# Degrees from the ends of runs instead of 64 counting passes, edge words on GpSimd, two sets of rank words

## The chip, the cores and the metric

The kernel runs on one core of one Trainium2 chip. A core has a matmul engine (TensorE, PE in the profile, with its weight load PEld), a vector engine (VectorE, DVE), a scalar engine (ScalarE, ACT), GpSimd (POOL) and a queue engine (SyncE, SP); 16 DMA engines move data between its on-chip memory and HBM. The metric is the device time of one execution in microseconds.

## The reference

A graph network of two layers runs over 6250 nodes with 128 features and 100,000 edges. Each edge has a source, a destination and one of 32 edge types, each node one of 16 node types. The edges come sorted by destination. `h` starts as `x`; each of the two layers computes

```python
k = typed_linear(h, ntype, Wk).reshape(n, H, HS)     # 16 weight sets, by node type
q = typed_linear(h, ntype, Wq).reshape(n, H, HS)
v = typed_linear(h, ntype, Wv).reshape(n, H, HS)
kT = jnp.einsum('nhd,htdo->nhto', k, Watt)           # 32 edge types
vT = jnp.einsum('nhd,htdo->nhto', v, Wmsg)
a = jnp.einsum('ehd,ehd->eh', kT[src, :, etype], q[dst]) * pri[:, etype].T / SQRT_D
att = edge_softmax(a, dst, n)                        # softmax over the edges of one destination
hag = segment_sum(vT[src, :, etype] * att, dst)
h = layernorm(gated(silu(typed_linear(hag, ntype, Wa)), h))
```

and the output is `layernorm(x + h @ ff_w + ff_b)`. There are 8 heads of 16 features.

## The kernel before

The kernel makes, for each layer, a table in HBM with one row of 256 floats (K and V) for every pair of node and edge type. Then it treats nodes in blocks of 128 with similar degrees: GpSimd gathers, edge slot by edge slot, one table row for each of the 128 nodes (L1310), and VectorE does the softmax and the sums. So three stages follow each other: layer 0's table; layer 0's edges with layer 1's table beside them; layer 1's edges. The change touches the first stage alone.

**Start (L316 to L468).** The edges lie in on-chip tiles of 128 partitions by 782 columns (`dsti`, `srci`, `eti`), partition by partition in their sorted order. The nodes are sorted by type with one-hot words and matmuls (L372 to L431), which gives `inv`, the list by which x is fetched. Beside that, VectorE makes the edge words `kvi = src * 32 + etype` (L448), the word by which a table row is named later, and checks that destinations do not fall along the edges (`falls`, L451 to L455) and that no partition spans 64 or more destinations (L457 to L460). A branch (L575) takes another path for unsorted edges; it isn't taken here. Its condition is read by every engine.

**Layer 0's table.** For each node type in turn (`linears0`, L952) GpSimd fetches blocks of x (L947), TensorE transposes them, ScalarE copies the result, TensorE multiplies by this type's Wk and Wv, and ScalarE and VectorE copy K and V (L991, L989); VectorE also copies what two types share (L971). Then for each block of 128 nodes and each half of the 32 edge types `table_block` (L287) issues eight matmuls of 512 columns, copies each result into a tile `st` (L306 on ScalarE; a quarter on VectorE, L304, in the stages "gathers" and "done"), and GpSimd scatters the tile to the table (L1002): 128 rows of 4096 floats. There are 49 blocks and 98 scatters, and four `st` tiles.

**Ranking, beside the table.** A Python generator, `rank_order` (L644), is advanced between the half-blocks of the table (L1014 to L1030): one step at each half in most stages, three steps in two halves while it yields nothing, and one step in two halves in the stage "gathers". It has these parts:

- `degrees` (L513). Column by column of 64, VectorE compares all 782 destinations less the partition's lowest with a constant and sums the hits (L537, an instruction with an accumulator that is read by a second one). After each four columns the counts are split into two small parts (L543 to L546), and one-hot words are built: `ol` for the node's place in its block (L548), `oh` for its block, times the count parts (L551, L555). Four matmuls a group (L531) sum them over the partitions.
- a histogram of degrees and a serial chain of small steps between VectorE and TensorE (L672 to L766),
- ranks of all nodes, by one-hot words of 128 columns for each block (L781 to L797),
- rank words (L813 to L838): for each group of up to four blocks VectorE builds `ol` (L825), `oh` (L829) and `ov` (L833), and matmuls L837 sum them to what each rank holds. Each of these three tiles exists once.
- the stage "gathers": GpSimd fetches the edge words of each block (L869) and its rows of x (L881), and stores the rows in rank order (L878, L887).

**Order of the work.** GpSimd's instructions run as the program states them. For the other engines a planner orders the instructions by its own estimates, so an instruction of VectorE can stand far ahead of its place in the program; each engine then works strictly in that order and waits at its head.

## Time and profile before

| what | us |
|---|---|
| median of three runs | 3341.53 (3329.39 to 3342.41) |
| the profiled execution | 3345.07 |
| its span, from the first to the last instruction | 3343.3 |
| start to the branch | 0 to 44 |
| layer 0's table, first to last scatter | 60.7 to 637.9 |
| first gather of layer 0's edges | 656.4 |

| from 44 to 656 us | PE | DVE | ACT | POOL |
|---|---|---|---|---|
| busy us | 521.4 | 288.9 | 362.2 | 266.3 |

A row of the timeline has the start and the duration in us, the engine, the line, the operation, the tile written and those read, their shapes, the count, and in brackets how long the engine was idle before it and what ended that wait. A row of a group of instructions has line, engine, operation, tiles, shape and count, then the busy time in us, the mean of one in ns, and the idle time ahead of them. A row of the busy table by stage has the stretch and its length, then for each engine the busy time and the number of instructions, the mean granted clock of TensorE as a share, the mean share of the DMA engines in use, and GB/s moved. "PE busy" counts pipelined matmuls with modelled ends, so a TensorE that is always busy need not be at its peak.

### The profile page before, as it was taken

The page shows a single profiled execution, that of the slowest core. Times are in us where ns is not written, and L with a number is a line of the kernel's source. Part 1 is how long each engine was busy: PE and PEld are TensorE (multiplying, and loading weights), DVE is VectorE, ACT ScalarE, POOL GpSimd, SP SyncE. Part 2 cuts the span into 40 slices and gives each one's busy share as a digit, 9 for nine tenths or more (in the row PEclk, how much of TensorE's full clock was granted, in tenths as well). Part 3 has the DMA queues.
Part 4 walks back from the last instruction along what each step waited for, and adds up shares of the span by engine and source line. Part 5 has one row for each costly group of instructions (what it writes and reads, how often), then busy time and mean ns, then how long its engine had stood idle before and what let it go on. Part 6 is the DMA issues. An engine that isn't in the chain of part 4 may idle for free. (4 is left out here: it accounts for less than half of the span.)

```text
span 3343.3 us, 22057 instructions
## 1 busy us (share of the span) xinstructions
PE 1738.2 (52%) x5612; PEld 808.2 (24%) x5612; DVE 1938.7 (58%) x4025; ACT 1014.6 (30%) x1677; POOL 2159.0 (65%) x2213
## 2 busy tenths in 40 slices
PE   3798998611874678766777677301212122122213
PEld 1344444400332323332332223101101111011111
DVE  8756332146646776666656653246556666666765
ACT  2575655400432235424342355101111121011111
POOL 2233665377577776777677563477767777777773
PEclk9679777555775777777777777655555555555655
DMA  7697999953675667757786588833333333333331
GB/s 200 255 391 304 401 399 406 382 111 101 214 244 196 217 231 285 253 192 248 266 290 217 170 299 341 296 108 104 101 93 103 101 101 101 101 103 99 100 101 44
DMA packets 194482, 691.09 MB, mean 207 GB/s; under 512 B 55469, under 2 KB 106032, under 8 KB 169298
## 3 DMA queue, kind: packets, MB, share of 16 engines
q0 software_dynamic: 119120, 651.15, 55.3%
q1 hardware_dynamic: 58838, 31.29, 3.5%
q10 hardware_dynamic: 16384, 7.11, 1.0%
q8 instruction: 48, 0.79, 0.1%
q14 instruction: 92, 0.75, 0.1%
HBM read 264.91 MB, written 429.48 MB: 208 GB/s over the span
## 5 line engine op out<-in xcount | busy, mean ns | idle before, releaser
L1310 POOL DMA_INDIRECT kv<-tab,ell x1734 | 1734.4, 1000 | 578.6 <-issue 451.5
L306 ACT COPY st<-tb 128x512 f32<-128x512 f32 (+1 forms) x1064 | 722.1, 758 | 396.8 <-PE tb L299 252.2
L284 PE MATMUL nb<-ident,hag 128*128 128x128 f32 x100 | 24.5, 379 | 750.5 <-DVE hag L1358 750.5
L1322 DVE TENSOR_TENSOR kv<-kv,q 128x896 f32<-128x896 f32 (+4 forms) x135 | 136.7, 1014 | 434.8 <-DMA kv<-tab,ell 410.9
L1322 DVE TENSOR_TENSOR kv<-kv,tb 128x768 f32<-128x768 f32 (+4 forms) x134 | 135.9, 1014 | 409.5 <-DMA kv<-tab,ell 356.2
L299 PE MATMUL tb<-bdv,vT 32*128 32x512 f32 x784 | 291.4, 862 | 32.9 <-ACT st L306 23.1
L299 PE MATMUL tb<-bdv,kvT 32*128 32x512 f32 x800 | 268.4, 823 | 53.6 <-ACT st L306 53.1
L299 PE MATMUL tb<-bdk,kvT 32*128 32x512 f32 x800 | 260.6, 818 | 56.1 <-ACT st L306 55.8
L1326 DVE TENSOR_REDUCE a<-kv 128x48 f32<-128x768 f32 (+4 forms) x269 | 269.7, 1003 | 1.5
L1002 POOL DMA_INDIRECT tab<-st,rows x98 | 103.5, 1056 | 240.5 <-ACT st L306 195.6
L278 PE MATMUL nb<-xm,wa 128*128 128x384 f32 (+1 forms) x384 | 201.9, 689 | 103.6 <-DVE xm L269 103.6
L299 PE MATMUL tb<-bdk,kT 32*128 32x512 f32 x784 | 250.9, 850 | 0.0
L1521 POOL DMA_INDIRECT tab<-st,row x100 | 104.2, 1042 | 177.1 <-ACT st L306 121.4
L304 DVE COPY st<-tb 128x512 f32<-128x512 f32 (+1 forms) x120 | 89.0, 744 | 205.3 <-PE tb L299 131.9
L284 PEld LDWEIGHTS nb<-ident,hag 128*128 128x128 f32 x100 | 14.8, 188 | 767.2 <-issue 552.5
L278 PE MATMUL nb<-xm,wq 128*128 128x384 f32 (+1 forms) x192 | 104.4, 705 | 136.0 <-DVE xm L269 136.0
L269 DVE SCALAR_TENSOR_TENSOR xm<-ntb,nb 128x384 f32<-128x384 bf16 (+1 forms) x240 | 132.1, 592 | 40.9 <-PE nb L284 28.0
L1206 ACT ACTIVATE tb<-a 128x128 f32<-128x128 f32 (+15 forms) x50 | 14.5, 289 | 435.8 <-DVE a L1203 435.8
L1454 PE MATMUL nb<-xm,wkqv 128*128 128x384 f32 (+1 forms) x288 | 125.5, 592 | 40.8 <-DVE xm L269 35.4
L278 PEld LDWEIGHTS nb<-xm,wa 128*128 128x128 f32 x384 | 94.0, 255 | 206.5 <-DVE xm L269 123.9
L1473 PE MATMUL nb<-xm,wkqv 128*128 128x384 f32 (+1 forms) x288 | 134.1, 626 | 14.0 <-DVE xm L269 14.0
L299 PEld LDWEIGHTS tb<-bdv,vT 32*128 32x128 f32 x784 | 108.8, 239 | 120.8 <-ACT st L306 92.3
(331 smaller groups left out, 2813.7 us busy)
## 6 DMA issues: line engine op xcount, KB each, us to landing
kv<-tab,ell POOLq DMA_INDIRECT x1734
hr<-xrd SPq DMA_DIRECT2D x21, 192.0 KB, 4.2
xrd<-xr POOLq DMA_DIRECT2D x11, 256.0 KB
hr<-xrd SPq DMA_DIRECT2D x10, 256.0 KB, 5.7
hrd<-hs SPq DMA_DIRECT2D x10, 192.0 KB, 2.2
qrd<-q SPq DMA_DIRECT2D x10, 192.0 KB, 6.8
tab<-st,row POOLq DMA_INDIRECT x100
tab<-st,rows POOLq DMA_INDIRECT x98
```

The source lines that it names most:

```text
L269: nc.vector.scalar_tensor_tensor(xm[:, :n], ntb[:, :n], float(t), hT[:, :n], op0=ALU.is_equal, op1=ALU.mult)
L278: nc.tensor.matmul(ps[:, :n], w[:, t, :], xm[:, :n], start=(t == types[0]), stop=(t == types[-1]))
L299: nc.tensor.matmul(pt[:, b], yT[s, i * P:(i + 1) * P], bd[s, tt, :], start=True, stop=True)
L304: nc.vector.tensor_copy(to, pt)
L306: nc.scalar.copy(to, pt)
L1002: put = nc.gpsimd.indirect_dma_start(out=tabs[0].rearrange("(n t) c -> n (t c)", t=16), out_offset=bass.IndirectOffsetOnAxis(ap=rows1[:, t ...
L1310: get = nc.gpsimd.indirect_dma_start(out=kv[:, j - j0, :], out_offset=None, in_=tabs[l][:], in_offset=bass.IndirectOffsetOnAxis(ap=ell[:, ...
L1322: nc.vector.tensor_tensor(kk, kk, q.unsqueeze(1).to_broadcast([P, c, D]), op=ALU.mult)
L1326: nc.vector.tensor_reduce(a[:, j0:j1, :], kk.rearrange("p k (h d) -> p k h d", h=H), axis=AX.X, op=ALU.add)
L1454: nc.tensor.matmul(outs[j][:, :n], wkqv[:, j, t, :], xm[:, :n], start=(t == types[0]), stop=(t == types[-1]))
L1473: nc.tensor.matmul(ps[:, :n], wkqv[:, j, t, :], xm[:, :n], start=(t == types[0]), stop=(t == types[-1]))
L1521: put = nc.gpsimd.indirect_dma_start(out=tabs[1].rearrange("(n t) c -> n (t c)", t=16), out_offset=bass.IndirectOffsetOnAxis(ap=row2[:, tg ...
```

## The change

It has three parts, all in the first stage.

1. `degrees` looks for the ends of runs. Each edge gets a key, `dst * 1024 + column + 1`; keys of edges whose successor has the same destination become 0. Eight times VectorE takes the eight largest keys of a partition and, but for the last time, replaces them by 0. Of the 64 keys found, the high bits are the nodes, and the differences of the low bits of neighbours are the degrees. They are split once for all, and one-hot words are built from bf16 operands as before, in 16 groups. The generator yields 44 times in this part instead of 35.
2. The edge words and the differences of neighbouring destinations are made on GpSimd in four instructions; VectorE takes the minimum of the differences. Behind the branch GpSimd makes the differences once more (the other path changes `dsti`) and numbers the columns.
3. Rank words have two sets of tiles, taken in turn, and the matmuls of a group are issued after the words of the next.

```diff
-    nc.vector.scalar_tensor_tensor(kvi, srci, float(RT), eti, op0=ALU.mult, op1=ALU.add)
-    falls = pp.tile([P, EC], F32, name="falls", tag="lo")
-    nc.vector.tensor_tensor(falls[:, :EC - 1], dsti[:, :EC - 1], dsti[:, 1:], op=ALU.is_gt)
-    nc.vector.tensor_tensor(falls[:, EC - 1:], dsti[:, EC - 1:], nxt, op=ALU.is_gt)
+    nc.gpsimd.tensor_scalar(kvi, srci, float(RT), None, op0=ALU.mult)
+    nc.gpsimd.tensor_tensor(kvi, kvi, eti, op=ALU.add)
+    rise = pp.tile([P, EC], I32, name="rise", tag="lo")
+    nc.gpsimd.tensor_tensor(rise[:, :EC - 1], dsti[:, 1:], dsti[:, :EC - 1], op=ALU.subtract)
+    nc.gpsimd.tensor_tensor(rise[:, EC - 1:], nxt, dsti[:, EC - 1:], op=ALU.subtract)
     nfalls = pp.tile([P, 2], F32, name="nfalls")
-    nc.vector.tensor_reduce(nfalls[:, 0:1], falls, axis=AX.X, op=ALU.add)
+    nc.vector.tensor_reduce(nfalls[:, 0:1], rise, axis=AX.X, op=ALU.min)
+    nc.vector.tensor_scalar(nfalls[:, 0:1], nfalls[:, 0:1], 0.0, None, op0=ALU.is_lt)
...
     def degrees(got):
-        rel = pp.tile([P, EC], F32, name="rel", tag="lo")
-        nc.vector.tensor_scalar(rel, dsti, lowest, None, op0=ALU.subtract)
...
+        last = pp.tile([P, EC], F32, name="last_at", tag="lo")
+        nc.vector.scalar_tensor_tensor(last, dsti, float(ROOM), nth, op0=ALU.mult, op1=ALU.add)
+        nc.vector.scalar_tensor_tensor(last[:, :EC - 1], rises[:, :EC - 1], 1.0, last[:, :EC - 1],
+                                       op0=ALU.min, op1=ALU.mult)
         yield
+        found = pp.tile([P, NEAR], F32, name="ends")
+        for r in range(0, NEAR, 8):
+            nc.vector.max(out=found[:, r:r + 8], in_=last)
+            if r + 8 < NEAR:
+                nc.vector.match_replace(out=last, in_to_replace=found[:, r:r + 8],
+                                        in_values=last, imm_value=0.0)
+            yield "degrees"
...
-        for c0 in range(0, NEAR, SB):
-            for c in range(c0, c0 + SB):
-                nc.vector.tensor_scalar(same, rel, float(c), None, op0=ALU.is_equal, op1=ALU.add,
-                                        accum_out=near[:, c:c + 1])
-                if c % 2:
-                    yield "degrees"
-            sl = slice(c0, c0 + SB)
-            neari = pp2.tile([P, SB], I32, name="neari")
-            nc.vector.tensor_copy(neari, near[:, sl])
...
+        for c0 in range(0, NEAR, G):
+            sl = slice(c0, c0 + G)
+            ol = pp2.tile([P, G, P], BF16, name="oc")
+            nc.vector.tensor_tensor(ol, at[:, 0, sl].unsqueeze(2).to_broadcast([P, G, P]),
+                                    colb.unsqueeze(1).to_broadcast([P, G, P]), op=ALU.is_equal)
+            yield "degrees"
...
+    rises = pp.tile([P, EC], I32, name="rises", tag="srci")
+    nc.gpsimd.tensor_tensor(rises[:, :EC - 1], dsti[:, 1:], dsti[:, :EC - 1], op=ALU.subtract)
+    nth = pp.tile([P, EC], F32, name="nth", tag="eti")
+    nc.gpsimd.iota(nth, pattern=[[1, EC]], base=1, channel_multiplier=0,
+                   allow_small_or_imprecise_dtypes=True)
...
-            for i0, k in superblocks(NT):
+            def said(i0, k, ol, ov):
+                for i in range(k):
+                    nc.tensor.matmul(say_ps, ol[:, i, :], ov[:, i], start=(i0 + i == 0),
+                                     stop=(i0 + i == NT - 1))
+            ready = None
+            for n, (i0, k) in enumerate(superblocks(NT)):
                 sl = slice(i0, i0 + k)
-                ol = pp2.tile([P, SB, P], F32, name="rl", bufs=1)
+                ol, oh, ov = (
+                    pool.tile([P, SB, *w], F32, name=f"say_{tag}", tag=tag, bufs=1)
+                    for (pool, tag), w in zip(
+                        ((pp, "srci"), (pp, "eti"), (pp, "lo")) if n % 2 else
+                        ((pp2, "rl"), (pp2, "rh"), (pp2, "rv")), ((P,), (NB,), (4, NB))))
...
-                for i in range(k):
-                    nc.tensor.matmul(say_ps, ol[:, i, :], ov[:, i], start=(i0 + i == 0),
-                                     stop=(i0 + i == NT - 1))
+                if ready:
+                    said(*ready)
+                ready = i0, k, ol, ov
                 yield
+            said(*ready)
```

More of the change, by code (lines that the diff above doesn't have):

```diff
@@ L527, in degrees @@
+        nc.vector.tensor_copy(nearb, nears)
+        yield "degrees"
         deg_ps = pps.tile([P, 2, NT], F32, name="ps")
+        G = SB
         def products(c0, ol, oh):
-            for c in range(c0, c0 + SB):
+            for c in range(c0, c0 + G):
                 nc.tensor.matmul(deg_ps, ol[:, c - c0, :], oh[:, c - c0],
@@ L560, in degrees @@
             ready = c0, ol, oh
-        yield "degrees"
+            yield "degrees"
         products(*ready)
```

50 lines of the change are left out of this document (27 added, 23 removed).

## The prediction

> **What bounds the kernel now.** I read the page first, then the busy table by stage, then the scatter issues in the timeline, then the groups of instructions. The page's span, shares and transfer rates:
>
> ```profile
> span 3343.3 us, 22057 instructions
> PE 1738.2 (52%) x5612; PEld 808.2 (24%) x5612; DVE 1938.7 (58%) x4025; ACT 1014.6 (30%) x1677; POOL 2159.0 (65%) x2213
> GB/s 200 255 391 304 401 399 406 382 111 101 214 244 196 217 231 285 253 192 248 266 290 217 170 299 341 296 108 104 101 93 103 101 101 101 101 103 99 100 101 44
> ```
>
> No engine is full over the span, so only the stage that is changed counts: the first eight slices of 83.6 us, where 98 scatters write layer 0's table. Its end is fixed by the last scatter and its landing (L1002), because layer 0's first gather (L1310) waits for it:
>
> ```profile
> L1002 POOL DMA_INDIRECT tab<-st,rows x98: 974/1017/2214, 60.7 to 637.9; - x98
> ...
> 656.38 1.01 POOL L1310 DMA_INDIRECT kv<-tab,ell  x1 [17.55 <-DMA tab<-st,rows]
> ```
>
> From there on the instruction order of the changed program is that of the old one on every engine. So what the stage wins or loses up to 656 us is carried one to one to the end of the span. The stage in four stretches (columns: busy time and count for PE, PEld, DVE, ACT, POOL; then granted clock, DMA share, GB/s):
>
> ```profile
> 61.00:178.00 117.00, 90.66 (x369) 41.08 (x368) 85.05 (x274) 72.30 (x144) 32.64 (x38) 0.71 0.72 295
> 178.00:277.00 99.00, 94.30 (x519) 47.43 (x518) 67.88 (x143) 71.83 (x142) 29.18 (x32) 0.83 0.94 388
> 277.00:318.00 41.00, 35.23 (x167) 19.96 (x165) 27.70 (x92) 22.59 (x44) 11.55 (x11) 1.00 0.62 253
> 318.00:656.00 338.00, 290.33 (x971) 148.29 (x971) 93.55 (x156) 189.69 (x371) 185.62 (x200) 0.67 0.98 396
> ```
>
> The last stretch is bound by the transfers: 396 GB/s at a share of 0.98 makes 404 GB/s when full, and one scatter (128 rows of 4096 floats, 2.10 MB) takes 5.2 us. The transfers stood idle for 0.28 x 117 = 32.8, 0.06 x 99 = 5.9, 0.38 x 41 = 15.6 and 0.02 x 338 = 6.8 us, 61 us in all. That is the most that any work on the stage after the first scatter can win. The first stretch is the counting of degrees, the third the rank words.
>
> In the first stretch four scatters leave between 60.7 and 74.43, 4.6 us apart; then comes a hole, and the DVE row shows why: the copy of the second node type's V (L989), which the next table block needs, stood in the queue behind counting passes.
>
> ```profile
> 55.38 0.69 DVE L989 COPY vT<-l 128x512 f32<-128x512 f32 x1 [0.54 <-PE l L986]
> 74.43 1.01 POOL L1002 DMA_INDIRECT tab<-st,rows  x1 [2.59 <-DVE same_dst L537]
> 88.46 0.69 DVE L989 COPY vT<-l 128x512 f32 x1
> 93.71 1.02 POOL L1002 DMA_INDIRECT tab<-st,rows  x1 [16.51 <-ACT st L306]
> 177.64 0.99 POOL L1002 DMA_INDIRECT tab<-st,rows  x1 [2.17 <-ACT st L306]
> ```
>
> **The change, part by part.** Degrees, removed and added, from the groups of the stage (busy, mean ns, idle before):
>
> ```profile
> L537 DVE TENSOR_SCALAR_CACHE_REDUCE same_dst<-rel 128x782 bf16<-128x782 f32 x64 | 61.6, 963 | 0.7
> L555 DVE TENSOR_TENSOR rhb<-rhb,nears 128x196 bf16<-128x196 bf16 x32 | 11.5, 360 | 0.7
> L548 DVE TENSOR_TENSOR oc<-nidat,colf 128x512 bf16<-128x512 f32 x16 | 11.0, 688 | 15.7 <-PE ps L531 15.6
> L531 PE MATMUL ps<-rhb,oc 128*128 128x98 bf16 x64 | 6.8, 243 | 22.2 <-DVE rhb L555 22.2
> L551 DVE TENSOR_TENSOR rhb<-nidat,colf 128x196 bf16<-128x196 f32 x16 | 5.7, 354 | 0.0
> L537 DVE DVE_READ_ACCUMULATOR same_dst<-rel 128x1 f32 x64 | 5.2, 82 | 0.0
> L543 DVE CAST neari<-near 128x4 int32<-128x4 f32 x16 | 2.9, 182 | 0.3
> ```
>
> Before, VectorE did 61.6 + 5.2 of counting, 11.5 + 11.0 + 5.7 of one-hot words and three small conversions in each of 16 blocks (about 8.5): 103 us. After, it forms the keys in two passes (1.9), makes 8 maxima searches and 7 replacements over the same 782 columns, some 12 small splits (2.0) and the same 16 blocks of words (28.2). Neither search form is in this trace. From below, a pass over 782 columns costs 0.96 (L537); from above, a pass that carries a value from element to element costs 1.78:
>
> ```profile
> 16.02 1.78 DVE L390 TENSOR_TENSOR_SCAN sums_t<-ones,sums_t 128x784 f32<-128x784 f32 x1
> ```
>
> I take 1.0, nearer the counting pass, which also streams all columns and keeps a little: 15 us, 47 in all, 56 us of VectorE work less. Of that only what holds the scatters counts. In the changed order the second type's V copy stands behind all eight searches, the splits and two blocks of words. VectorE gets past the first type's V (the copy at 55.38) at about 57 us, as before; then about 10 us of searches, 2 of splits and 5 of words with copies and dependencies between them (about 2) put that copy at 76 instead of 88.46. The scatter follows 5 us later, at 81 instead of 93.71: **13 us won**. From there to the scatter at 177.64 there were 13 intervals in 83.9 us; without counting they take 13 x 5.2 = 68, or 75 if a half-clocked TensorE shows now and then (below). I take 71: **another 13 won**. The sum of 26 leaves 7 of the 32.8 us of idle transfers, for type changes and the first scatters.
>
> **Rank words.** Before, one block was a closed loop (L825, L833, then the matmuls L837, then L825 again):
>
> ```profile
> 287.18 1.62 PE L837 MATMUL ps<-rv,rl 128*128 128x200 f32 x8 [0.63 <-DVE rv L833]
> 288.73 1.13 PE L299 MATMUL tb<-bdk,kT 32*128 32x512 f32 x4
> 288.84 0.69 DVE L825 TENSOR_TENSOR rl<-partf,colf 128x512 f32<-128x512 f32 x1 [1.31 <-PE ps L837]
> 289.45 0.98 DVE L833 TENSOR_TENSOR rv<-rh,say 128x800 f32<-128x800 f32 x1
> 290.46 0.32 DVE L829 TENSOR_TENSOR rh<-partf,colf 128x150 f32<-128x150 f32 x1
> ...
> 292.03 1.14 PE L299 MATMUL tb<-bdv,vT 32*128 32x512 f32 x8
> ```
>
> With two sets of words and the products one block late, TensorE no longer waits 0.63 in each of 13 blocks: 8.2 us. The table's matmuls are no longer cut into halves there: 13 pieces become 9, and a half costs as much as a whole (1.13 against 1.14): 4.5 us. VectorE's own 0.69 + 0.32 + 0.98 = 2.0 a block, 26 in all, fits below what is left of the 41 us, but shares its queue with type copies. I take **10 us won** of 12.7; ends 4 (only the pieces joined) and 13.
>
> **Edge words and checks on GpSimd.** VectorE loses the passes L448 and L452 at the start, and no longer waits there for the edge types:
>
> ```profile
> 4.63 0.97 DVE L452 TENSOR_TENSOR falls<-dsti 128x781 f32<-128x781 int32 x1 [0.79 <-DMA dsti<-in_dst_dram]
> 11.28 0.97 DVE L448 SCALAR_TENSOR_TENSOR kvi<-srci,eti 128x782 int32<-128x782 int32 x1 [2.02 <-DMA eti<-in_edge_type_dram]
> 14.93 1.03 DVE L389 COPY sums_t<-tb 128x392 f32<-128x392 f32 x2
> 199.13 0.46 POOL L966 MEMSET kT<- 128x382 f32 x1
> ```
>
> But the minimum of the rises waits for GpSimd's last piece, and stands ahead of L389 and of everything that leads to the first fetch of x. GpSimd's price for 782 columns: one stream as the memset has it gives 0.94; two inputs and an output as three such streams give 2.8. I take two streams, 1.9. The Trainium skill (GPSIMD Engine Reference, section 4.1 Engine selection) speaks against this part: elementwise work belongs on VectorE, GpSimd being about twice as slow with two inputs. By its figures (section 3.1) an estimate is 1.7 us a pass, and the sum would not move by 0.5 us; no row here shows such a pass. The edge types land at 11.28, the addition ends at 13.2, the minimum at 14.4: L389 starts 0.5 sooner than now. Behind it VectorE has two blocks of degree words and some splits less, about 1.5 us. After the branch, the rises are made again and columns numbered on GpSimd, ahead of the second fetch of x in its queue: 1.9 + 0.9 = 2.8 later. I count nothing in sum; with the ends 0.94 and 2.8 it is 3 won to 4 lost.
>
> **Moved work at no cost.** The degree part has nine steps more, so ranking ends nine half-blocks later: gathers of edge words and x rows (L869, L881) begin five scatters later and end three scatters before the last, not seven. Their cover is the full transfer queue of the last stretch. If it goes, the wait of the last row store is exposed:
>
> ```profile
> 612.77 0.80 POOL L887 DMA_DIRECT2D xrd<-xr  x1 [8.60 <-DMA xr<-in_x_dram,some]
> ```
>
> Three scatters stand behind it then; the queue held 17.55 us of work after the last scatter, so 8.6 stays covered. SP's and ACT's queues keep their order but for copies.
>
> **Sum.** 13 + 13 + 10 = 36, less 1 for what a fuller transfer queue can no longer take in: 35 us. The profiled execution took 3345.07 and becomes 3310; it lies 3.5 us above the median of the runs shown, so the median becomes 3341.5 - 35 = 3307.
>
> **Rivals.** (a) TensorE's clock falls while it waits for transfers, and the degree stage runs at the half-clock pace:
>
> ```profile
> 132.00:140.00 8.00, 8.00 (x32) 3.71 (x32) 3.02 (x10) 5.67 (x11) 3.52 (x4) 0.50 0.77 312
> 160.00:178.00 18.00, 18.00 (x94) 8.79 (x91) 7.09 (x26) 17.55 (x37) 6.87 (x9) 1.00 1.01 418
> ...
> 131.66 1.01 POOL L1002 DMA_INDIRECT tab<-st,rows  x1 [3.87 <-ACT st L306]
> 137.82 1.01 POOL L1002 DMA_INDIRECT tab<-st,rows  x1 [3.87 <-ACT st L306]
> ```
>
> At clock 0.50 scatters are 6.16 us apart with these degree matmuls between. Thirteen such intervals are 80, not 71: 3316. Against it: a TensorE without a pause got 1.00 again by 160. [...] (b) Transfers never idle behind the first scatter: 58 won, 3283; against it, type changes and the serial steps between ranks stay. (c) Slower: the searches cost more than a pass. Each us on the price delays the second V copy by 15 us. At 1.78 the time is 3319; the gain is gone at 3.3 us a search; at 4.5 the kernel is slower by 0.5%; at 6, 3382. For it: no row prices these forms; against it: every other pass of this width costs 1.8 or less. (d) GpSimd's passes are far slower: above 2.8 us, each us more delays minimum and fetches by about 4.5; at 8 us, 27 are lost and the time is 3334, no measurable change. (e) The change gives nothing because transfers fill the time anyway, 3341: the 0.98 speaks for it, the 0.72 and 0.62 against.
>
> **How the numbers follow.** A run of this kernel can be told from no change beyond about 0.5%, 17 us. Chances: forecast 0.58, (a) 0.16, (b) 0.07, (c) beyond 2 us 0.09, (d) 0.05, (e) 0.05. Faster: the first three and little more, 0.80; the same: (d), (e) and a fringe of (c), 0.11; slower: the rest of (c), 0.09. The range takes (a), (b), and (d) up to no gain: 3283 to 3335; the forecast's own is 3295 to 3320.
>
> **What would show it.** The scatter now at 93.71 at about 81; that at 177.64 near 150; DMA share from 61 to 150 above 0.9; blocks of rank words 2.5 us apart, not 3.3; searches of about 1 us; the first gather of layer 0 at about 621. Wrong: searches over 3 us, a late minimum ahead of the type counting, or a granted clock of 0.5 in the degree stage.

## The result and the profile after

The changed kernel takes 3311.61 us (median of 8 runs, 3301.43 to 3320.38), the kernel before, run beside it, 3340.44 (8 runs, 3329.39 to 3348.8): a ratio of 0.9918, 95% interval 0.9895 to 0.994. That is 28.8 us less by the medians. The profiled execution of the changed kernel took 3308.28, its span fell by 36.8 us. The page of the changed kernel, as for the kernel before:

```profile
span 3306.5 us, 21912 instructions
PE 1715.2 (52%) x5612; PEld 795.9 (24%) x5612; DVE 1890.3 (57%) x3877; ACT 1013.5 (31%) x1677; POOL 2165.7 (65%) x2219
GB/s 172 403 412 340 400 406 411 279 94 103 278 221 194 181 248 285 253 200 258 270 292 177 217 305 312 290 108 104 102 92 103 101 102 101 102 102 99 99 101 44
```

VectorE lost 48.4 us of busy time and TensorE 23.0, and the second slice went from 255 to 403 GB/s. The busy table of the changed kernel over the same four stretches:

```profile
61.00:178.00 117.00, 113.76 (x466) 53.56 (x458) 48.93 (x127) 95.47 (x190) 40.69 (x46) 0.83 0.93 383
178.00:277.00 99.00, 95.23 (x543) 49.49 (x542) 69.84 (x146) 73.92 (x148) 30.60 (x33) 0.88 0.96 397
277.00:318.00 41.00, 35.94 (x174) 22.10 (x174) 31.11 (x103) 23.86 (x48) 15.64 (x16) 0.83 0.74 299
318.00:656.00 338.00, 267.12 (x896) 132.49 (x891) 96.36 (x152) 169.83 (x334) 200.26 (x213) 0.68 0.99 379
```

The DMA share of the first stretch rose from 0.72 to 0.93, of the third from 0.62 to 0.74 only. In bytes, by two rows of the same view for before and then two for the changed kernel:

```profile
61.00:277.00 216.00, 184.96 (x887) 88.50 (x886) 152.93 (x416) 144.13 (x285) 61.82 (x69) 0.76 0.82 338
277.00:350.00 73.00, 61.81 (x271) 32.61 (x271) 43.05 (x121) 41.32 (x81) 30.05 (x30) 0.91 0.73 294
```

```profile
61.00:277.00 216.00, 208.98 (x1008) 103.05 (x1000) 118.78 (x273) 169.39 (x337) 71.28 (x79) 0.85 0.94 390
277.00:350.00 73.00, 64.65 (x296) 36.93 (x296) 42.44 (x121) 46.69 (x92) 37.02 (x40) 0.85 0.86 348
```

By 350 us the kernel before had moved 216 x 0.338 + 73 x 0.294 = 94.5 MB, the changed kernel 84.2 + 25.4 = 109.6 MB. The 15.1 MB between them are 37 us at the 404 GB/s of a full queue: the gain of this pair of profiles (36.8 us of span) is transfers that no longer wait.

Scatters and the first gather in the timeline of the changed kernel (scatters are counted from 0; those that the prediction calls by 93.71 and 177.64 are scatter 4 and scatter 17):

```profile
66.30 1.03 POOL L1036 DMA_INDIRECT tab<-st,rows  x1 [7.35 <-ACT st L308]
...
84.22 1.02 POOL L1036 DMA_INDIRECT tab<-st,rows  x1 [1.44 <-ACT st L308]
...
151.42 1.50 POOL L1036 DMA_INDIRECT tab<-st,rows  x1 [4.27 <-ACT st L308]
...
594.12 0.80 POOL L921 DMA_DIRECT2D xrd<-xr  x1 [8.18 <-DMA xr<-in_x_dram,some]
...
597.85 0.97 POOL L1036 DMA_INDIRECT tab<-st,rows  x1 [0.30 <-issue]
617.90 1.01 POOL L1344 DMA_INDIRECT kv<-tab,ell  x1 [19.08 <-DMA tab<-st,rows]
```

The wait of 16.51 us ahead of scatter 4 is gone (1.44). But scatter 0 starts at 66.30 instead of 60.72. The stage, split at scatters (us, both columns read from the timelines):

| from | to | before | after | won |
|---|---|---|---|---|
| start | scatter 0 | 60.72 | 66.30 | -5.6 |
| scatter 0 | scatter 4 | 32.99 | 17.92 | 15.1 |
| scatter 4 | scatter 17 | 83.93 | 67.20 | 16.7 |
| scatter 17 | scatter 22 | 26.23 | 27.99 | -1.8 |
| scatter 22 | scatter 44 (rank words) | 143.50 | 131.71 | 11.8 |
| scatter 44 | first gather | 309.01 | 306.78 | 2.2 |
| first gather | end of the span | 2686.9 | 2688.6 | -1.7 |

So there are two gains, in the degrees and in the rank words, and one loss that the prediction had put at nothing: the start.

### The profile page after: what moved, and what is told of

Its sections match the earlier page's. It is cut to its first block, busy times and chain, and to the rows that moved or that the text cites. A ratio compares the mean times of both kernels' runs of the same rounds, so it can differ in the third digit from the quotient of the medians.

```text
span 3306.5 us, 21912 instructions
## 1 busy us (share of the span) xinstructions
PE 1715.2 (52%) x5612; PEld 795.9 (24%) x5612; DVE 1890.3 (57%) x3877; ACT 1013.5 (31%) x1677; POOL 2165.7 (65%) x2219
## 5 line engine op out<-in xcount | busy, mean ns | idle before, releaser
L301 PE MATMUL tb<-bdk,kT 32*128 32x512 f32 x784 | 221.3, 836 | 1.6 <-DVE st L306 1.6
L286 PEld LDWEIGHTS nb<-ident,hag 128*128 128x128 f32 x100 | 15.1, 191 | 766.3 <-issue 550.4
L301 PEld LDWEIGHTS tb<-bdv,vT 32*128 32x128 f32 x784 | 116.1, 229 | 127.7 <-ACT st L308 100.0
```

The source lines that it names most:

```text
L301: nc.tensor.matmul(pt[:, b], yT[s, i * P:(i + 1) * P], bd[s, tt, :], start=True, stop=True)
```

## The experiments

All ratios are to the kernel before, run beside the others on the same chip; its median there was 3343.66 us for degrees_only to words_on_vector, 3340.14 for after_again to spread_words and 3348.95 for the last four, so medians of different groups are not compared directly. The stage's times of every profile in one place (us; "rest" is span less first gather; the last columns are the median of all runs of that kernel and its ratio). The names are explained one by one below; after_again is the changed kernel without an edit.

| kernel | scatter 0 | 4 | 22 | 44 | first gather | rest | median | ratio, 95% |
|---|---|---|---|---|---|---|---|---|
| before | 60.72 | 93.71 | 203.87 | 347.37 | 656.38 | 2686.9 | 3340.44 | 1 |
| changed | 66.30 | 84.22 | 179.41 | 311.12 | 617.90 | 2688.6 | 3311.61 | 0.9918 (0.9895 to 0.994) |
| degrees_only | 61.91 | 81.44 | 173.01 | 318.06 | 624.87 | 2691.1 | 3320.55 | 0.9949 (0.9929 to 0.9969) |
| words_only | 60.80 | 93.81 | 204.00 | 334.68 | 643.47 | 2683.1 | 3328.45 | 0.9964 (0.995 to 0.9977) |
| gpsimd_only | 62.33 | 94.52 | 201.13 | 336.71 | 647.85 | 2684.6 | 3338.42 | 0.9997 (0.9983 to 1.0012) |
| words_on_vector | 61.48 | 81.00 | 172.53 | 305.67 | 612.88 | 2690.9 | 3311.49 | 0.9924 (0.9902 to 0.9946) |
| after_again | 66.00 | 83.62 | 181.93 | 320.92 | 628.23 | 2689.0 | 3316.48 | 0.9925 (0.9905 to 0.9945) |
| twice_max | 66.55 | 88.24 | 185.01 | 314.90 | 621.82 | 2684.3 | 3308.90 | 0.9908 (0.9893 to 0.9924) |
| rises_on_vector | 64.38 | 82.01 | 175.60 | 308.68 | 615.32 | 2690.6 | 3308.18 | 0.9914 (0.9889 to 0.994) |
| spread_words | 64.89 | 82.51 | 182.10 | 307.31 | 616.72 | 2683.0 | 3301.52 | 0.9888 (0.987 to 0.9906) |
| rise_only_gpsimd | 64.08 | 81.70 | 179.76 | 318.71 | 625.46 | 2694.1 | 3321.39 | 0.992 (0.99 to 0.9941) |
| edge_words_only_gpsimd | 61.91 | 79.54 | 184.73 | 316.42 | 623.55 | 2687.6 | 3308.26 | 0.9881 (0.9858 to 0.9904) |
| spread_on_vector | 63.14 | 82.52 | 186.50 | 310.41 | 620.38 | 2688.3 | 3305.46 | 0.9867 (0.9844 to 0.9889) |
| spread_all_on_vector | 60.94 | 80.46 | 178.43 | 301.79 | 611.48 | 2688.7 | 3301.99 | 0.9876 (0.9852 to 0.99) |

The rest after the first gather stays within 2683 to 2694 whatever is done to the stage, and follows no edit. Two profiles of one and the same kernel, changed and after_again, differ by 0.3 us at scatter 0 and by 10.3 at the first gather. So a difference of a few us between two single profiles says something at scatter 0, and little at the first gather.

### The three parts one at a time

The kernel before with the degree part alone (rises and column numbers behind the branch included):

```diff
 # the changed kernel, with edge words, the order test and rank words of before
-    nc.gpsimd.tensor_scalar(kvi, srci, float(RT), None, op0=ALU.mult)
-    nc.gpsimd.tensor_tensor(kvi, kvi, eti, op=ALU.add)
+    nc.vector.scalar_tensor_tensor(kvi, srci, float(RT), eti, op0=ALU.mult, op1=ALU.add)
...
-                if ready:
-                    said(*ready)
-                ready = i0, k, ol, ov
+                for i in range(k):
+                    nc.tensor.matmul(say_ps, ol[:, i, :], ov[:, i], start=(i0 + i == 0),
+                                     stop=(i0 + i == NT - 1))
```

> The kernel before with the degree part alone (keys, maxima searches, words from bf16; the two helper instructions behind the branch on GpSimd come with it); edge words stay on VectorE, rank words are single. My theory: the counting passes held the second node type's V copy and starved TensorE, so this part alone brings 24 to 28 us less 3 for the helpers ahead of the fetches: 21 to 25 us faster than before; the scatter number 17 (from 0) near 150 us, but blocks of rank words still 3.3 us apart. Rival, the transfers fill the time anyway: less than 6 us faster. Rival, the parts only win together because transfers then catch up at the rank words: 10 to 15 us.

Measured: 0.9949, 17 us of 3343.66 by the ratio and 23 by the medians, so its theory (21 to 25) and its last rival (10 to 15) can't be told apart by the time; the first rival is out. From scatter 0 to 22 it takes 111.1 us instead of 143.15, 32 less, nearly as the changed kernel (113.1). Scatter 17 leaves at 145.22, sooner than the 150 expected.

The kernel before with the new rank words alone:

```diff
-                ol = pp2.tile([P, SB, P], F32, name="rl", bufs=1)
+                ol, oh, ov = (
+                    pool.tile([P, SB, *w], F32, name=f"say_{tag}", tag=tag, bufs=1)
...
+                if ready:
+                    said(*ready)
+                ready = i0, k, ol, ov
```

> The kernel before with two sets of rank words alone. My theory: TensorE's wait of 0.63 us in each of 13 blocks goes and the table's matmuls are no longer cut: blocks 2.5 us apart instead of 3.3, 8 to 12 us faster than before. Rival, transfers lag there anyway and take the gain back later: 0 to 3 us. Start and degree stage as before.

Measured: 0.9964, 12 us by the ratio, 15 by the medians. All scatters up to the 28th stay where they were; scatter 44 comes 12.7 us sooner, the first gather 12.9.

The kernel before with the four GpSimd instructions at the start alone:

```diff
-    nc.vector.scalar_tensor_tensor(kvi, srci, float(RT), eti, op0=ALU.mult, op1=ALU.add)
+    nc.gpsimd.tensor_scalar(kvi, srci, float(RT), None, op0=ALU.mult)
+    nc.gpsimd.tensor_tensor(kvi, kvi, eti, op=ALU.add)
...
-    nc.vector.tensor_reduce(nfalls[:, 0:1], falls, axis=AX.X, op=ALU.add)
+    nc.vector.tensor_reduce(nfalls[:, 0:1], rise, axis=AX.X, op=ALU.min)
```

> The kernel before with the edge words and the check of order on GpSimd alone. My prediction counted this part at nothing, 3 us won to 4 lost. By the changed kernel's trace the type counting starts at 15.80 instead of 14.93 us behind the minimum, so 1 us slower is what the start alone gives; if the 2.9 us longer branch of the changed kernel (from the condition to the next instruction 4.6 instead of 1.5 us) belongs to this part, 4 us slower. Rival, GpSimd's words free VectorE at the start: 1 to 2 us faster. The degree stage keeps its hole before scatter 4.

Measured: 0.9997, nothing that can be told from no change, with scatter 0 at 62.33 instead of 60.72. By the ratios (1 less ratio, times the kernel before) the parts are 17 + 12 + 1 = 30 us and the whole is 27. By the medians they are 23 + 15 + 5 = 43 against 29, and at the first gather of the profiles 31.5 + 12.9 + 8.5 = 53 against 38.5. So each of the first two parts wins by itself; whether the parts add up isn't shown.

### What the GpSimd part costs at the start

The changed kernel with edge words and order test back on VectorE:

```diff
-    nc.gpsimd.tensor_scalar(kvi, srci, float(RT), None, op0=ALU.mult)
-    nc.gpsimd.tensor_tensor(kvi, kvi, eti, op=ALU.add)
+    nc.vector.scalar_tensor_tensor(kvi, srci, float(RT), eti, op0=ALU.mult, op1=ALU.add)
...
-    nc.gpsimd.tensor_tensor(rise[:, :EC - 1], dsti[:, 1:], dsti[:, :EC - 1], op=ALU.subtract)
...
+    nc.vector.tensor_tensor(falls[:, :EC - 1], dsti[:, :EC - 1], dsti[:, 1:], op=ALU.is_gt)
...
```

> The changed kernel with one part undone: edge words and the check of order back on VectorE. If GpSimd's words cost the start about 1 us and nothing else, it is 0 to 2 us faster than the changed kernel (31 us faster than before); if the longer branch belongs to GpSimd's words, 4 us faster than the changed kernel. Rival, they win what they take off VectorE: 1 to 2 us slower than the changed kernel. Either way the degree and word parts alone keep nearly the whole gain.

Measured: scatter 0 at 61.48, 4.8 us sooner, and the first gather 5.0 sooner, but a median of 3311.49 (0.9924): within the spread of runs this is the changed kernel's own time. 5 us are 0.15%, less than these medians tell apart. Type counting starts at 14.45 (15.80 in the changed kernel). Where the rest of the 4.8 us goes is seen in the timelines. First the changed kernel's, around the branch (the condition `nfi`, then the next work of VectorE and GpSimd):

```profile
42.22 0.14 DVE L468 CAST nfi<-ps 1x1 int32<-1x1 f32 x1 [0.43 <-PE ps L466]
...
46.83 0.17 DVE L724 CAST rc<-rci 128x2 f32<-128x2 int32 x1 [4.21 <-DVEq L593]
47.03 1.39 DVE L726 TENSOR_SCALAR sameclass<-cc,rc 128x128 f32<-128x128 int32 x1
```

```profile
46.83 1.51 POOL L661 TENSOR_TENSOR rises<-dsti 128x781 int32<-128x781 int32 x1 [3.54 <-DVEq L593]
48.30 0.81 POOL L663 IOTA nth<- 128x782 f32 x1
49.28 1.70 POOL L981 DMA_INDIRECT wkqv<-in_x_dram,inv  x1 [0.17 <-issue]
```

Then VectorE of the kernel before:

```profile
42.58 0.15 DVE L464 CAST nfi<-ps 1x1 int32<-1x1 f32 x1 [0.43 <-PE ps L462]
...
44.07 0.63 DVE L516 TENSOR_SCALAR rel<-dsti,lowest 128x782 f32<-128x782 int32 x1 [1.09 <-DVEq L575]
```

From the condition to VectorE's next instruction it is 1.5 us there, 1.5 in words_on_vector (41.24 to 42.73) and 4.6 in the changed kernel. The second fetch of x is issued at 49.28 in the changed kernel and takes 1.70; GpSimd of the kernel before:

```profile
44.88 0.96 POOL L947 DMA_INDIRECT wkqv<-in_x_dram,inv  x1 [1.32 <-DVE rel L516]
```

Not every engine waits longer. By the view of the branch's line, GpSimd's own queue has its next event 0.5 us behind its branch instruction in all fourteen profiles, and the branch instruction of TensorE's weight loads takes 4.0 to 4.5 us in all of them, with either length on VectorE. In the changed kernel it is GpSimd's first instruction behind the branch, `rises`, that waits for VectorE's queue (`<-DVEq L593`). gpsimd_only, which has the same order test but no `rises`, shows the difference, VectorE first and then GpSimd's second fetch:

```profile
42.96 0.14 DVE L466 CAST nfi<-ps 1x1 int32<-1x1 f32 x1 [0.43 <-PE ps L464]
...
47.43 0.63 DVE L518 TENSOR_SCALAR rel<-dsti,lowest 128x782 f32<-128x782 int32 x1 [4.08 <-DVEq L577]
```

```profile
45.26 0.96 POOL L949 DMA_INDIRECT wkqv<-in_x_dram,inv  x1 [1.23 <-remote]
```

VectorE's branch is long there too, 4.5 us, but the second fetch follows the condition by 2.3 us, as in the kernel before (42.58 to 44.88). In words_on_vector, with `rises` but the short branch, it follows by 4.1 us (41.24 to 45.37), in the changed kernel by 7.1. So the late second fetch takes both: the long branch of VectorE, and an instruction ahead of the fetch on GpSimd that waits for VectorE.

Two more runs split the GpSimd part in halves. In the first the order test's differences stay on GpSimd:

```diff
-    nc.gpsimd.tensor_scalar(kvi, srci, float(RT), None, op0=ALU.mult)
-    nc.gpsimd.tensor_tensor(kvi, kvi, eti, op=ALU.add)
+    nc.vector.scalar_tensor_tensor(kvi, srci, float(RT), eti, op0=ALU.mult, op1=ALU.add)
```

> The changed kernel, with the edge words (one VectorE pass) back on VectorE and the differences behind the order test still on GpSimd. Between the condition of the branch and VectorE's next instruction lay 1.5 us in every kernel with neither on GpSimd and 4.1 to 4.8 us in every kernel with both. If the handing over from GpSimd to VectorE (the order test's minimum) makes the branch long, it is 4 us or more here, and the first scatter starts near 65; if the edge words do it (two passes, and the store behind them that then waits for GpSimd), it is 1.5 us, and the first scatter starts near 62. If it is only how long GpSimd is busy ahead of the branch (7.7 us with both, 3.7 here), it lies between. Time: 3305 to 3316.

in the second the edge words do:

```diff
-    nc.gpsimd.tensor_tensor(rise[:, :EC - 1], dsti[:, 1:], dsti[:, :EC - 1], op=ALU.subtract)
-    nc.gpsimd.tensor_tensor(rise[:, EC - 1:], nxt, dsti[:, EC - 1:], op=ALU.subtract)
+    nc.vector.tensor_tensor(falls[:, :EC - 1], dsti[:, :EC - 1], dsti[:, 1:], op=ALU.is_gt)
+    nc.vector.tensor_tensor(falls[:, EC - 1:], dsti[:, EC - 1:], nxt, op=ALU.is_gt)
...
```

> The changed kernel, with the order test's differences back on VectorE (as falls) and the edge words still on GpSimd: the mirror of the run before. Branch of 4 us or more and a first scatter near 65 if the edge words and their store make it long; 1.5 us and near 62 if the order test does; in between if it is GpSimd's busy time (4.0 us here). Type counting starts near 14.5, as where both are on VectorE, if VectorE's own falls are no dearer than the wait for GpSimd's (15.8 with both on GpSimd). Time: 3305 to 3316.

VectorE around the branch, first with the differences alone on GpSimd, then with the edge words alone:

```profile
41.21 0.15 DVE L467 CAST nfi<-ps 1x1 int32<-1x1 f32 x1 [0.43 <-issue]
...
45.87 0.15 DVE L721 TENSOR_SCALAR rci<-rowi 128x1 int32<-128x1 int32 x1 [4.26 <-DVEq L592]
46.06 1.32 DVE L723 CAST rc<-rci 128x2 f32<-128x2 int32 x1
```

```profile
41.67 0.14 DVE L467 CAST nfi<-ps 1x1 int32<-1x1 f32 x1 [0.43 <-PE ps L465]
...
43.17 0.15 DVE L737 TENSOR_SCALAR few<-rc 128x1 f32<-128x1 f32 x1 [1.09 <-DVEq L592]
```

4.7 us against 1.5: VectorE's long branch goes with the order test on GpSimd, not with the edge words, their store or the time for which GpSimd is busy. Over all profiles this holds without exception (4.1 to 4.8 us in the seven kernels whose minimum is taken over GpSimd's differences, 1.5 in the seven others). That is not yet a cause. GpSimd's last piece ends 27 us ahead of the condition in the changed kernel and 33 us ahead in rise_only_gpsimd (7.72 to 41.21), and the edit also turns VectorE's sum into a minimum and a comparison. Another reading fits as well: in the seven kernels with the long branch 117 to 124 instructions of VectorE run ahead of it, in the seven others 95 to 109. No run separates these. Scatter 0 came as expected (64.08 and 61.91, expected near 65 and 62); of the times, both expected at 3305 to 3316, 3308.26 did and 3321.39 didn't. Type counting starts at 14.75 and 14.89, so each half by itself gives back most of what both cost there (15.80). The medians of these two kernels, three executions each, lie 13 us apart, and the 2.2 us at scatter 0 don't explain that; their profiles differ by 8.4, of which 6.5 lie behind the first gather, where the edit can't reach by its order.

The work that stands behind the branch on GpSimd was tried by itself:

```diff
-    nc.gpsimd.tensor_tensor(rises[:, :EC - 1], dsti[:, 1:], dsti[:, :EC - 1], op=ALU.subtract)
+    nc.vector.tensor_tensor(rises[:, :EC - 1], dsti[:, 1:], dsti[:, :EC - 1], op=ALU.subtract)
```

> The changed kernel with the differences behind the branch made on VectorE instead of GpSimd, so that GpSimd has only the column numbers (0.8 us) ahead of the second fetch of x. The fetches and the first scatter come 1.5 us sooner; 1 to 2 us faster than the changed kernel if the start reaches the end one to one. Rival, the first scatter waits for something else, or VectorE's extra pass takes it back: 0.

Scatter 0 starts at 64.38, 1.9 us sooner than in the changed kernel; the time of 3308.18 can't be told from it.

### Whether the searches' price matters

Each search for maxima made twice, the first result thrown away:

```diff
+            nc.vector.max(out=spare8, in_=last)
             nc.vector.max(out=found[:, r:r + 8], in_=last)
```

> The changed kernel with each of the eight maxima searches made twice (the first result is thrown away): 8 us more of VectorE work ahead of the second node type's V copy, nothing else. My rival (c) said that each us on the price of a search delays that copy by its whole sum. Path: the copy comes at 86 instead of 78 us, scatter number 4 at 90 or 91 instead of 84, and 4 to 8 us of it reach the end. Rival, the scatters have slack there because the copy was no longer the last thing they waited for: 0 to 2 us.

Measured: 3308.9, where the changed kernel beside it (after_again) took 3316.48: the 4 to 8 us expected aren't seen, and the rival's 0 to 2 fits. Eight more searches cost VectorE 7.8 us, and the second V copy starts at 82.70 instead of 78.24, not at 86. Scatters 4 and 8 of that kernel:

```profile
88.24 1.02 POOL L1038 DMA_INDIRECT tab<-st,rows  x1 [0.17 <-ACT st L308]
...
110.68 1.02 POOL L1038 DMA_INDIRECT tab<-st,rows  x1 [1.82 <-ACT st L308]
```

Scatter 4 is 4.0 us later than in the changed kernel (84.22), scatter 8 at 110.68 only 1.0 later (109.70). Scatters 1 to 4 are 2.6 to 4.0 us late, and by the eighth most of it is made up. Behind that the two profiles part again (scatter 17 is 7.7 us later, the first gather 3.9), at a granted clock of 0.54 from 132 to 152 us in this one and 0.83 in the changed kernel's first. In this kernel 1 us more for each search of maxima costs nothing that can be told.

### The same kernel once more: the clock

The changed kernel without an edit:

> The changed kernel as it is, in the same call as the next three so that they can be compared on one chip. 25 to 33 us faster than the kernel before; its branch again 4.6 us from the condition to the next instruction if that belongs to the kernel and not to one execution.

Measured: 3316.48 (0.9925), 23.7 us below the kernel before by the medians and 25 by the ratio, where 25 to 33 were expected. VectorE's branch is long again, 4.5 us. This profile's span is 3317.2, 10.7 more than the first one's. The largest difference begins in the stretch from 105 to 132 us, here of the first profile and then of this one:

```profile
105.00:132.00 27.00, 27.00 (x132) 12.68 (x129) 11.61 (x31) 25.27 (x51) 11.50 (x13) 1.00 1.01 414
```

```profile
105.00:132.00 27.00, 27.00 (x94) 13.14 (x97) 7.58 (x20) 18.64 (x37) 9.87 (x11) 0.51 0.85 343
```

At a granted clock of 0.51 TensorE, busy all the time in both, does 94 matmuls instead of 132. Four scatters (8 to 12) take 25.8 us instead of 17.5. But the first profile has its own stretch at a low clock, a little later; the first profile and then this one:

```profile
152.00:182.00 30.00, 30.00 (x120) 14.62 (x118) 9.90 (x33) 21.99 (x44) 9.66 (x11) 0.65 1.00 418
```

```profile
152.00:182.00 30.00, 29.15 (x148) 13.50 (x146) 12.43 (x37) 27.87 (x56) 10.43 (x15) 1.00 1.01 421
```

There the DMA engines stay full at either clock. From 105 to 152 us this execution moves 2.9 MB less than the first (343 against 414 GB/s to 132, then 370 against 421), 7 us of a full queue, and from 222 to 264 us another 1.8 MB less (374 against 417 GB/s, at clocks of 0.88 and 0.99), 4.5 us. So a low clock goes with lost transfers in some stretches and not in others. The first gather comes 10.3 us later. By 350 us this execution had moved 216 x 0.376 + 73 x 0.330 = 105.3 MB, 4.3 MB or 11 us less than the first, by rows of the same two stretches:

```profile
61.00:277.00 216.00, 207.49 (x958) 98.78 (x954) 112.11 (x260) 163.95 (x326) 70.59 (x76) 0.81 0.91 376
277.00:350.00 73.00, 67.21 (x325) 38.76 (x321) 47.92 (x131) 46.80 (x92) 33.33 (x35) 0.89 0.82 330
```

What sets the clock in one execution and not in the next, with the same instructions, isn't shown by anything here; TensorE is busy for the whole of both slow stretches.

### Spreading the rank words, and the best of both

In the changed kernel scatters 38 to 44 are still 6.3 to 11 us apart (from 263.30 to 311.12), because the generator gives one rank-word group after the other, three steps in two halves, while the transfers could take more. The next kernel gives one step at each half there, and takes the room from the degrees:

```diff
             nc.vector.tensor_tensor(ol, at[:, 0, sl].unsqueeze(2).to_broadcast([P, G, P]),
                                     colb.unsqueeze(1).to_broadcast([P, G, P]), op=ALU.is_equal)
-            yield "degrees"
...
                 ready = i0, k, ol, ov
-                yield
+                yield "words"
```

> The changed kernel with the ranking advanced differently: one step less in each of the 16 groups of degree words (so ranking comes 8 scatters sooner), and one step in each half-block while rank words are made, instead of three in two. In the changed kernel the scatters at the rank words are 6.3 to 11 us apart (five of 7 us) and the transfers stand idle for about 11 us of 41. Theory: the blocks of rank words then share the table's time, scatters 5.5 to 6 us apart, 5 to 9 us faster than the changed kernel. Rival, VectorE's degree words in half the time hold the table instead: 0 or slower.

Measured: 3301.52 (0.9888, 0.987 to 0.9906), 15 us below the changed kernel beside it (0.9905 to 0.9945), more than the 5 to 9 expected. Its two stretches, as above:

```profile
61.00:277.00 216.00, 202.46 (x1051) 102.73 (x1049) 145.82 (x367) 163.27 (x325) 72.40 (x78) 0.88 0.91 377
277.00:350.00 73.00, 66.60 (x249) 34.08 (x245) 24.83 (x40) 47.07 (x91) 48.91 (x56) 0.73 0.99 397
```

81.4 + 29.0 = 110.4 MB by 350 us: the share behind 277 us is 0.99 now, but the hole has moved to before it (0.91 instead of 0.94), and ranking ends sooner: the first gather of edge words is issued at 265.03 instead of 297.58. That is 0.8 MB, 2 us, more than the changed kernel's first profile and 5.1 MB, 12.6 us, more than its second. So the edit's share of the 15 us lies somewhere between next to nothing and nearly all; two profiles of the one kernel and one of the other can't say how much is the clock's.

Last, both findings in one kernel, without and with the rises behind the branch on VectorE:

```diff
 # spread_words, and:
-    nc.gpsimd.tensor_scalar(kvi, srci, float(RT), None, op0=ALU.mult)
-    nc.gpsimd.tensor_tensor(kvi, kvi, eti, op=ALU.add)
+    nc.vector.scalar_tensor_tensor(kvi, srci, float(RT), eti, op0=ALU.mult, op1=ALU.add)
...
+    nc.vector.tensor_reduce(nfalls[:, 0:1], falls, axis=AX.X, op=ALU.add)
...
 # spread_all_on_vector, besides:
-    nc.gpsimd.tensor_tensor(rises[:, :EC - 1], dsti[:, 1:], dsti[:, :EC - 1], op=ALU.subtract)
+    nc.vector.tensor_tensor(rises[:, :EC - 1], dsti[:, 1:], dsti[:, :EC - 1], op=ALU.subtract)
```

> The changed kernel with three edits: the edge words and the order test's differences back on VectorE, one turn less for each group of the degree loop, and the rank words' loop giving way at each half of a type. The two edits of the scheduling alone gave 3301.5 us (0.9888), the one on VectorE alone brought the first gather from 617.9 to 612.9 but no time that could be told from the changed kernel's. If what the stage wins carries to the end, the first gather starts near 612 and the time is 3296 to 3299. If the 5 us at the start are taken back where the transfers are full (as the times of the two single runs say), it is 3300 to 3303 and the gather near 616.

> The run before, with the differences behind the branch on VectorE as well, so that GpSimd holds only the count of columns ahead of the second fetch. The first fetch's start was 1.9 us sooner for this edit on the changed kernel, which had the long branch; VectorE gets some 1.0 us more ahead of the first scatter. First scatter near 61 (61.5 without the edit), first gather 610 to 614 and 3294 to 3299 if the start carries to the end; the same time as the run before if it doesn't.

Measured: 3305.46 and 3301.99 on a chip on which the kernel before took 3348.95: ratios 0.9867 and 0.9876. Both times missed the numbers expected; that chip is slower by 0.26%, or 8.8 us, than the one of spread_words, which is about the size of the misses. Against the kernel before they gain 43.5 and 47.0 us by the medians. The first one's interval (0.9844 to 0.9889) lies below the changed kernel's 0.9895 to 0.994, the second's (0.9852 to 0.99) overlaps it a little. Against spread_words (0.9888) they can't be told apart. spread_on_vector has its first gather at 620.38, later than the 612 and the 616 expected; spread_all_on_vector has scatter 0 at 60.94 and the first gather at 611.48, as expected and the earliest of all. Their first scatters are 2.2 us apart, where 0.5 was expected: 0.4 are there at the condition already (41.86 and 41.49), and 1.8 at the second fetch (45.99 and 44.15).

## Why the prediction held, step by step

**The time.** 3307 was predicted and 3311.6 measured, inside the forecast's own 3295 to 3320. The sum, made for one execution, said 35; the profiled pair lost 36.8 us of span, the medians 28.8. The 8 us between these two are those of the profiled executions: the kernel before's took 4.6 us more than its median, the changed kernel's 3.3 less. The sum had allowed for the first, as 3.5. One other profile of the changed kernel (after_again) is 10.7 us longer and has low clocks in other places, which is rival (a) in part; whether that is what spreads the medians isn't shown.

**The carry to the end** was right: 38.5 us at the first gather, 36.8 at the end of the span.

**Degrees: price right.** The groups of the changed kernel from 44 to 300 us:

```profile
L564 DVE TENSOR_TENSOR oc<-endat,colb 128x512 bf16<-128x512 bf16 x16 | 11.0, 689 | 20.5 <-PE ps L557 20.5
L573 DVE TENSOR_TENSOR rhb<-ends_same,nearb 128x196 bf16<-128x196 bf16 x32 | 10.1, 358 | 0.0
L526 DVE MAX8 ends<-last_at 128x8 f32<-128x782 f32 x8 | 7.8, 974 | 0.2
L528 DVE MATCH_REPLACE8 last_at<-ends,last_at 128x782 f32<-128x782 f32 x7 | 6.7, 957 | 0.0
L569 DVE TENSOR_TENSOR ends_same<-endat,colb 128x196 bf16<-128x196 bf16 x16 | 5.7, 360 | 0.4
L528 DVE MATCH_VALUE_LOAD last_at<-ends,last_at 128x8 f32 x7 | 0.6, 89 | 0.2
```

The searches cost 7.8 + 6.7 + 0.6 = 15.1 us, 15 were taken. With 26.8 of words, 1.9 of keys and about 2 of splits it is 46, predicted 47. A search took 974 ns and a replacement 957, the counting pass 963.

**Degrees: 13 and 13.** The two V copies of the changed kernel:

```profile
60.01 0.69 DVE L1023 COPY vT<-l 128x512 f32<-128x512 f32 x1 [0.79 <-PE l L1020]
...
78.24 0.68 DVE L1023 COPY vT<-l 128x512 f32 x1
```

VectorE is past the first at 60.7 instead of 57, 3.7 us late. The second follows 17.5 us later, where 19 were predicted, and scatter 4 comes 6.0 us behind that copy instead of 5. So it left at 84.22, not 81: 9.5 won instead of 13. Scatter 17 left at 151.42, near 150: 26.2 won, 26 predicted. The pace from scatter 4 to 17 was 67.2 / 13 = 5.17 us, full transfers. The 71 allowed for a half clock now and then; the clock was 0.71 from 84 to 105 us and 0.83 from 132 to 152, and the scatters kept the pace of a full queue all the same. So that 26 came out is luck, two errors of opposite sign: the degree part wins 30 to 32 us from scatter 0 to 22 (degrees_only: 32), and the start loses 5.6.

**Edge words and checks on GpSimd, counted at nothing: this step failed.** The start of the changed kernel, GpSimd and then VectorE:

```profile
9.29 2.19 POOL L450 TENSOR_SCALAR kvi<-srci 128x782 int32<-128x782 int32 x1 [6.52 <-DMA srci<-in_src_dram]
11.46 1.48 POOL L455 TENSOR_TENSOR rise<-dsti 128x781 int32<-128x781 int32 x1
12.91 1.82 POOL L451 TENSOR_TENSOR kvi<-kvi,eti 128x782 int32<-128x782 int32 x1
14.70 0.18 POOL L456 TENSOR_TENSOR rise<-nxt,dsti 128x1 int32<-128x1 int32 x1
```

```profile
14.91 0.97 DVE L458 TENSOR_REDUCE nfalls<-rise 128x1 f32<-128x782 int32 x1 [6.32 <-POOL rise L456]
15.80 1.03 DVE L391 COPY sums_t<-tb 128x392 f32<-128x392 f32 x2
```

The passes cost 2.19, 1.48 and 1.82, inside the bounds of 0.94 to 2.8. But they come one after another, the differences' last piece behind both passes of the edge words, so the minimum starts at 14.91 and L391 at 15.80: 0.9 later than the 14.93 before, not 0.5 sooner. A late minimum ahead of the type counting was among the signs of being wrong, and it came. That is made good later: the condition comes at 42.22, before at 42.58. What the step missed lies behind it. VectorE's branch is 3.1 us longer (4.6 against 1.5), and GpSimd's `rises` wait for VectorE there. They and the column numbers take 2.4 us ahead of the second fetch, which before came 0.8 behind VectorE's first instruction. With the condition 0.36 sooner that is 3.12 + 1.64 - 0.36 = 4.40 us at the second fetch (49.28 against 44.88), where 2.8 was expected, and 5.6 at scatter 0. The fetch itself takes 1.70 instead of 0.96 us; why isn't shown. The price of a pass on GpSimd, the danger that rival (d) named, wasn't it: the wait behind the branch was in no term of the sum, and what makes that branch long stays open.

**Rank words: 10 predicted, 11.8 measured** (12.7 alone). The mechanism is the one foreseen: in the kernel before TensorE waited for words ahead of 12 of the 13 groups, and in the changed kernel's timeline ahead of the first alone. The waits before were 6.8 us in sum (ten of about 0.6 and two of 0.3), not 13 times 0.63. The last of the 13 groups begins at 295.07 and ends at 296.6, 32.7 us after the start of the first, or 2.5 us each. The 11.8 are those of one profile from scatter 22 to 44, with the histogram and the ranks in them; after_again took 139.0 us there instead of 131.71, at other clocks. The transfers still idle for 0.26 x 41 = 11 us of the stretch from 277 to 318 us; in spread_words the share from 277 to 350 us is 0.99.

**Moved gathers at no cost: right.** The wait of the last row store is 8.18 us and ends 3.7 us ahead of the last scatter, behind which 19.08 us of transfers are queued.

**The rivals.** (a) came in part, at the size given (26 us for four scatters, 6.5 each, against 6.16), but its condition, a TensorE that waits, is doubtful: in after_again's slow stretch it is busy for 27.00 of 27.00 us at a clock of 0.51. It had waited ahead of that (busy for 16.12 of 21 us from 84 to 105), and nearly as much in the first profile (17.76), where no such stretch followed at once. (b) didn't: 0.07 x 117 + 0.04 x 99 + 0.26 x 41 + 0.01 x 338 = 26 us of idle transfers are left. (c) had its law wrong, 15 us for each us on the price: twice_max adds 1 us to every maxima search and loses nothing that can be told; the copy comes 4.5 us later, not 8, and of the 4.0 us at scatter 4, 1.0 is left at scatter 8. Its other end, where the searches fill the stage, wasn't tried. (d)'s price didn't come (2.19 us at most in the changed kernel), and (e) is out.

## What to carry to other kernels

A transfer-bound stage with holes is priced by its holes: the bytes moved by 350 us gave the difference in span to 5 us here (37 against 36.8, 11 against 10.7, 2 against 6.8 for spread_words), while the 48 us of VectorE work removed did not. Work that is moved to GpSimd "at no cost" must be followed to what stands ahead of the next fetch in GpSimd's own queue, and to what that waits for. And two profiles of one kernel were 10 us apart with no edit between them, so an edit worth less than that needs medians of runs on one chip.

## What the runs showed of the hardware that wasn't expected

Small passes of VectorE lasted as long as the GpSimd pass that had begun before them. In the changed kernel `sameclass` (128 x 128) took 1.39 us from 47.03, while GpSimd's rises ran from 46.83 to 48.34; with the differences alone on GpSimd it was a conversion of 128 x 2 that took 1.32 us from 46.06, with the rises running beside it:

```profile
45.87 1.48 POOL L660 TENSOR_TENSOR rises<-dsti 128x781 int32<-128x781 int32 x1 [3.67 <-DVEq L592]
```

Both ended with GpSimd's pass, within 0.1 us. In the kernel before the first of them took this:

```profile
47.65 0.28 DVE L702 TENSOR_SCALAR sameclass<-cc,rc 128x128 f32<-128x128 int32 x1
```

Beside the column numbers it was 0.76 us (rise_only_gpsimd, from 47.48, the numbers from 47.31 to 48.10). The Trainium skill (SBUF — State Buffer, "SBUF: two separate sides") says that VectorE and GpSimd share one pair of ports: of a GpSimd instruction and a VectorE instruction that is in a 2-port mode or has two inputs in on-chip memory, whichever starts first holds the pair for its whole length and the other is blocked. These rows agree, 0.28 against 1.39 us; the mode of VectorE's instructions isn't in the profile.

From the condition of a branch that isn't taken to VectorE's next instruction it was 1.5 us in seven kernels and 4.1 to 4.8 in the seven whose order test goes through GpSimd; the branch instruction of TensorE's weight loads took 4.0 to 4.5 us in all fourteen, and GpSimd's next event came 0.5 us behind its own. And the clock that TensorE is granted, with the same instructions and TensorE without a pause, was 1.00 in one execution and 0.51 in another over the same 27 us.
